# A third pair of score buffers, lent from the projection banks, in the last unit of a decoder layer

## The chip, the cores and the metric

The kernel runs on one core of a Trainium2 chip. The metric is the device time of one launch in microseconds (us). All arithmetic is fp32.

## The reference

One decoder layer for x of 4 batches x 1024 tokens x 512 features, with 16 heads of 32 features. Three blocks follow each other, each with a layer norm in front and a residual after it: a gated self-attention, a cross-attention over a context of 384 features, and a small network of 64 units with 16 hidden values each.

```python
# gated self-attention (B, H, q, k)
attn = softmax(inner @ outer.T / sqrt(dh)) * aperture[..., None] * expression[..., None, :]
attn = attn / (attn.sum(-1) + 1e-8)
x = x + rotate(attn @ v) @ Wout
# cross-attention: q from layernorm(x), k and v from the context
attn = softmax(clip(q @ k.T * D ** -0.5, -1e4, 1e4))
x = x + (attn @ v) @ Wo + bo
# network
s = layernorm(x) @ Win + bin_
g = (relu(s[..., None] * W1 + b1) * W2).sum(-1) + b2
x = x + g @ Wout + bout
```

## The kernel before, in words

The work is cut into eight **units**: self-attention of the four batches, then cross-attention of the four batches. The last unit is the cross-attention of batch 3. A unit has two **halves** of 512 queries (hf). Each half runs 32 **steps**: four groups g of four heads, and in each group eight tiles kt of 128 keys. A step (`step`, `scores`, `times`) does the following, in program order on each engine:

- TensorE computes the scores of two pairs of heads (line 574). A pair fills a tile s of 128 partitions x 2 x 512 values in PSUM, which is two banks. The pool `ps` holds two such tiles. Each head's scores are two 32x64 matmuls (16 records in a trace for the step's eight matmuls).
- ScalarE makes one exponential e for each pair (line 579), 128x1024 values, into one of six buffers.
- VectorE adds e into es, the running sum for the softmax (lines 585 and 587). In the last unit only the first pair is summed there; the second pair's row sums are TensorE matmuls, sm (line 609), made every second step for two key tiles. In the very last group of the last half (`closing`) VectorE sums both pairs, and there is no sm.
- TensorE multiplies the exponentials of the step before with the values, av (line 601).

After the last key tile of a group, `normalize` copies av and sm to SBUF (lines 618 and 620), a step later `add_up` adds the sums across partitions (line 631, copied at line 632), and their way goes by DMA: sum_d, cs, then `divide` (lines 655 to 671) three steps later, rec_d, recb, and `multiply` (line 681) after three more steps.

The other work of a unit is placed between these steps by `run(main, items)`. It has a list of small parts, each with a cost c (about one projection part is 1; pauses have a cost and no work) and gives each step its share of the list by cost. `beside(u, hf)` writes the list by hand. In the last unit, for either half, it holds: pauses; the output projection of an earlier half (line 87, 16 parts, two per step); two outputs of the network of the half before that (line 879); pauses, among which stand the layer norm (root, lines 290 to 299; normalization, line 303), its transposition by way of DMA (rows_d, line 307; xn, line 312; VectorE's block transposes, line 318) and bias additions (line 826); the inputs of the network (line 841); and pauses again. The hidden values of the network (hid on ScalarE, line 862, and g on VectorE, line 868) are spread over the pauses and the projection parts; they have no cost in the list.

All these matmuls besides scores, av and sm write to single banks that `bank()` hands out from the pool `pf`, which holds two of them (tag f). With the two tiles of `ps` (four banks) and one bank each for av and sm, all eight banks of PSUM are given out. The order on each engine is the program's; every DMA named here stands on SP's queue in program order.

After the last step of the last half, the program goes on with the last output projection, norm and network, written out by hand.

Of the kernel before, what the change touches and what calls it, by code (L numbers as in the profile page):

```python
# [10 lines left out]
F32 = mybir.dt.float32  # L11
U32 = mybir.dt.uint32
AF = mybir.ActivationFunctionType
# [3 lines left out]
P = 128  # L17
# [8 lines left out]
HALF = 512  # L26
# [4 lines left out]
SCALE = 1.0 / math.sqrt(DH)  # L31
# [32 lines left out]
def moderate_path(tc: tile.TileContext, a: dict, out: bass.AP, flag: bass.AP):  # L64
    nc = tc.nc
    x = a["x"]
    with ExitStack() as st:
# [3 lines left out]
        ps = enter(tc.tile_pool(name="mps", bufs=2, space=bass.MemoryType.PSUM))  # L71
# [5 lines left out]
        p3 = enter(tc.tile_pool(name="mp3", bufs=3))  # L77
        p4 = enter(tc.tile_pool(name="mp4", bufs=4))

        def bank():  # L80
            return pf.tile([P, HALF], F32, tag="f", name="f")

        def columns(to, lhsT, rhs, **flags):

            for j in range(4):
                r = slice(j * DH, (j + 1) * DH)
                nc.tensor.matmul(to[r], lhsT=lhsT[:, j, :] if len(lhsT.shape) == 3 else lhsT[:, r], rhs=rhs, **flags)  # L87
# [249 lines left out]
        n = len(order)  # L337
# [213 lines left out]
        def attention(u, hf):  # L551

            ph, b = order[u]
# [9 lines left out]
            def closing(g):  # L563
                return (u, hf, g) == (len(order) - 1, 1, HG - 1)

            def scores(g, kt):
                q, k = me["q", hf], me["k"]
                es = []
                for i in range(2):
                    s = ps.tile([P, 2, HALF], F32, tag="s", name="s")  # L570
                    for j in range(2):
                        r = slice((2 * i + j) * DH, (2 * i + j + 1) * DH)
                        for m in range(0, P, 64):
                            nc.tensor.matmul(  # L574
                                s[m : m + 64, j, :], lhsT=k[r, g, kt * P + m : kt * P + m + 64], rhs=q[r, g, :],
                                start=True, stop=True,
                            )
                    e = p4.tile([P, 2, HALF], F32, tag="e", name="e", bufs=6)
                    nc.scalar.activation(e, s, AF.Exp, scale=SCALE)  # L579
                    es.append(e)  # L580
                me["e", kt] = es
                for i in range(1 if shared and not closing(g) else 2):
                    if kt == 1:
                        me.setdefault("es", {})[i] = p1.tile([P, 2, HALF], F32, tag=f"es{i}", name="es")
                        nc.vector.tensor_tensor(me["es"][i], me["e", 0][i], es[i], ALU.add)  # L585
                    elif kt > 1:
                        nc.vector.tensor_tensor(me["es"][i], me["es"][i], es[i], ALU.add)  # L587
                if ph == 0 and kt > 0:
                    if kt == 1:
                        me["eg"] = p1.tile([P, 2, HALF], F32, tag="es1", name="eg")  # L590
                    for h in range(2):
                        eg, gate = me["eg"][:, h, :], lambda t: me["sw"][:, t, HG * g + h, 1:2]
                        if kt == 1:
                            nc.vector.tensor_scalar(eg, me["e", 0][0][:, h, :], gate(0), None, ALU.mult)
                        nc.vector.scalar_tensor_tensor(eg, es[0][:, h, :], gate(kt), eg, ALU.mult, ALU.add)  # L595
                return es
# [131 lines left out]
        def post(u, hf):  # L728

            ph, b = order[u]  # L730
# [22 lines left out]
            def project(t):  # L753
                def part(cs, to=None):
                    def f():
                        assert last or me["divided", hf] >= cs[-1]
                        if cs[0] == 0:
                            res["po"] = to() if to else bank()
                            res["po", t] = res["po"]
                        if last:  # L760
                            res["po"] = res["po", t]
                        for c in cs:
                            columns(
                                res["po"], me["q", hf][:, c, ts(t, P)], me["wo", hf][:, c, :],
                                start=(c == 0), stop=(c == NC - 1),
                            )
                        if cs[-1] < NC - 1:
                            return
                        r = res[t]
                        nc.vector.tensor_tensor(r, res["po"], r, ALU.add)  # L770
                        s6 = p2.tile([P, 6], F32, tag="bnst1", name="bnst1")
                        if t == 0:
                            res["mv"] = p2.tile([P, 4, 2], F32, tag="fmv", name="fmv")
                        nc.vector.bn_stats(s6, r)
                        nc.vector.bn_aggr(res["mv"][:, t, :], s6)
                        if ph == 0:
                            r2 = p2.tile([P, D], F32, tag="r2", name="r2")
                            nc.gpsimd.tensor_tensor(r2, r, bo_bc, ALU.add)  # L778
                            nc.sync.dma_start(x1b_d[b][4 * hf + t], r2)
                    return len(cs), f  # L780
                if last:
                    return [part([0, 1, 2], (lambda: ps.tile([P, 2, HALF], F32, tag="s", name="s")[:, 0, :]) if t > 1 else None), part([3])]
                return [part([c]) for c in range(4)]
# [8 lines left out]
            def root(a=0, n=4):  # L792
                if ph == 1:
                    i = 2 * NS + b * NT + 4 * hf + a
                    nc.gpsimd.tensor_copy(marks[:, i : i + n], res["mv"][:, a : a + n, 1])
                rs = rsqrt(res["mv"][:, a : a + n, :], n)
                for t in range(n):
                    res["rs", a + t] = rs[:, t : t + 1]
                if last:
                    res["nm", a] = p2.tile([P, n], F32, tag="ve", name="nm")  # L800
                    nc.vector.scalar_tensor_tensor(res["nm", a], res["mv"][:, a : a + n, 0], -1.0, rs, ALU.mult, ALU.mult)

            def norm(t):
                def f():
                    if last:
                        if t == 0:
                            res["xn"] = p1.tile([P, 4, D], F32, tag="tok", name="xn")
                        to = res["xn"][:, t, :]
                        if t % 2:
                            nc.scalar.activation(  # L810
                                to, res[t], AF.Identity, bias=res["nm", t - 1][:, 1:2], scale=res["rs", t]
                            )
                        else:
                            normalized(to, res[t], res["mv"], res["rs", t], t)
                        return
                    r2 = p2.tile([P, 1, D], F32, tag="r2", name="r2")
                    normalized(r2[:, 0, :], res[t], res["mv"], res["rs", t], t)
                    away(rows_d[b][hf], r2, t, 1)
                return [(0, f)]
# [70 lines left out]
            def bout(t):  # L890
# [11 lines left out]
            r = {  # L902
                "wo": [[(0, fetch)]],
                "load": loads,
                "o": [project(t) for t in range(4)],
                "ln": ([[(0, lambda a=a: root(a, 2))] for a in (0, 2)] if last else [[(0, root)]])
                + [norm(t) for t in range(4)],
            }
# [21 lines left out]
                done = upto  # L930
            return [out + second[done:]]

        def run(main, items):

            parts = sum(items, [])
            total = sum(c for c, _ in parts)
            done = 0
            for n, f in enumerate(main):
                f()
                while parts and (done + parts[0][0] / 2 <= total * (n + 1) / len(main) or n == len(main) - 1):  # L940
                    c, f1 = parts.pop(0)
                    if f1:
                        f1()
                    done += c
# [4 lines left out]
        n = len(order)  # L949
# [87 lines left out]
        first += one(load_wout) + one(rotations) + p["gt"][1]  # L1037
        first += p["v"][1][0:3] + pres[1]["tr"][0] + p["v"][1][3:]
        run([lambda: None], first)
        for u in range(n):  # L1040
            if u == 0:
                crossing.append(True)
            for hf in range(2):
                run(attention(u, hf), beside(u, hf))
        tail = ending[0]
        sums, divide, look = settle(n - 1, 1, HG - 1)
        late.pop(0)()
# [5 lines left out]
        o, ln, b, tr, s = ([part for item in tail[k] for part in item] for k in ("o", "ln", "b", "tr", "s"))  # L1053
        h = [part for item in held[0]["h"] for part in item]
# [18 lines left out]
        h = sum(tail["h"], [])  # L1073
# [650 lines left out]
```

## Time and profile before

| | |
|---|---|
| median of 3 runs | 2200.21 us |
| lowest and highest | 2198.55, 2200.22 us |
| profiled execution, span from first to last instruction | 2198.2 us |
| TensorE busy | 2170.0 us (99%) |
| VectorE, ScalarE, GpSimd busy | 71%, 56%, 4% |
| mean granted TensorE clock | 0.997 |
| last unit's first step, last step | 1927.8 us, 2141.6 us from the start |

The profiled execution has no time besides its span: the three times given are those of the runs. Its span lies 2.0 us under their median. In the lines of a profile PE is TensorE, PEld its weight loads, DVE is VectorE, ACT is ScalarE, SPq are DMAs issued by SP; L574 is line 574 of the kernel; "x16" counts instructions; a bracket gives idle time just before an instruction and what ended it.

### The profile page before, as it was taken

Reading aid. Unit: us, or ns where it says so; the run is one execution under the profiler, and the core shown is the slowest. Engines: PE = TensorE matmul, PEld = TensorE weight load, DVE = VectorE, ACT = ScalarE, POOL = GpSimd, SP = SyncE. Lnnn points to the kernel's source line nnn. Section 1 sums busy time; section 2 is a strip of 40 time slices with the busy share of each in tenths; the row PEclk is TensorE's granted clock in tenths of the full one; section 3 lists DMA queues with packets and bytes.
Section 4 is the critical chain, followed back from the end, with each engine's and each line's share of the span. In section 5 each row is a group of like instructions: output and inputs, shape, how many; then the busy total and the mean of one; then the engine's idle time right before and its main releaser. Section 6 shows DMA issues by size and latency. Waiting matters only on the chain.

```text
span 2198.2 us, 52765 instructions
## 1 busy us (share of the span) xinstructions
PE 2170.0 (99%) x22606; PEld 551.7 (25%) x22606; DVE 1562.5 (71%) x2526; ACT 1237.6 (56%) x1489; POOL 82.2 (4%) x118
## 2 busy tenths in 40 slices
PE   8999999999999999999999999999999999999996
PEld 3322222222222222222222222222222222222223
DVE  4478675796757957567677676877777777856477
ACT  0155545555455554555656566675757666577673
POOL 1000000030210000000000000000000000000000
PEclk9999999999999999999999999999999999999998
DMA  4412123132231221211222132222234142213131
GB/s 141 131 61 55 63 96 106 29 88 66 97 104 31 82 69 47 68 57 42 70 85 90 45 89 69 79 70 59 69 84 112 46 107 69 61 39 80 59 89 41
DMA packets 153304, 161.70 MB, mean 74 GB/s; under 512 B 46202, under 2 KB 91898, under 8 KB 151908
## 3 DMA queue, kind: packets, MB, share of 16 engines
q1 hardware_dynamic: 149068, 156.14, 24.6%
q8 instruction: 179, 2.93, 0.6%
q0 software_dynamic: 2144, 0.98, 0.3%
q10 hardware_dynamic: 1848, 1.12, 0.2%
q14 instruction: 65, 0.53, 0.1%
HBM read 115.40 MB, written 42.74 MB: 72 GB/s over the span
## 4 chain that ended last, share of the span: by engine, by line
PE 93%; DVE 3%; DMA 1%; ACT 1%; issue 1%; SPq 0%; DVEq 0%; ACTq 0%
PE f L87 36%; PE s L574 25%; PE av L601 21%; PE sm L609 6%; PE sm L631 3%; ACT e L579 1%; DMA w<-in_attn_Wo 1%; PE f L841 1%; PE f L879 1%; DVE g L868 1%; DVE es L587 1%; DMA rows_d<-r 0%; PE s L879 0%; PE f L471 0%; DMA rec_d<-rec 0%
## 5 line engine op out<-in xcount | busy, mean ns | idle before, releaser
L579 ACT ACTIVATE e<-s 128x1024 f32<-128x1024 f32 x1024 | 993.4, 1022 | 709.9 <-PE s L574 512.9
L587 DVE TENSOR_TENSOR es<-es,e 128x1024 f32<-128x1024 f32 x534 | 642.2, 1227 | 253.6 <-ACT e L579 251.6
L574 PE MATMUL s<-q,k 32*64 32x512 f32 x8192 | 607.5, 613 | 2.2 <-ACT e L579 0.5
L601 PE MATMUL av<-e,v 128*32 128x512 f32 x4096 | 550.4, 603 | 0.0
L87 PE MATMUL f<-xT,w 128*32 128x512 f32 x2816 | 333.7, 592 | 0.6 <-PE f L87 0.6
L595 DVE SCALAR_TENSOR_TENSOR eg<-e,sw,eg 128x512 f32<-128x512 f32 x448 | 318.5, 746 | 2.3
L585 DVE TENSOR_TENSOR es<-e 128x1024 f32<-128x1024 f32 x89 | 106.7, 1223 | 216.4 <-ACT e L579 185.4
L574 PEld LDWEIGHTS s<-q,k 32*64 32x64 f32 x8192 | 132.9, 130 | 445.6 <-ACT e L579 242.2
L87 PE MATMUL f<-w,q 128*32 128x512 f32 x1984 | 240.3, 593 | 0.0
L601 PEld LDWEIGHTS av<-e,v 128*32 128x32 f32 x4096 | 88.2, 108 | 403.7 <-issue 401.2
L87 PEld LDWEIGHTS f<-xT,w 128*32 128x32 f32 x2816 | 92.3, 110 | 211.0 <-issue 204.2
L609 PE MATMUL sm<-e,sw 128*2 128x512 f32 x1024 | 133.3, 592 | 0.0
L87 PE MATMUL f<-w,xT 128*32 128x512 f32 x896 | 106.0, 592 | 0.6 <-DVE q L284 0.6
L87 PEld LDWEIGHTS f<-w,q 128*32 128x32 f32 x1984 | 65.8, 110 | 148.9 <-issue 141.5
L87 PE MATMUL f<-w,ctxT 128*32 128x512 f32 x768 | 92.6, 592 | 0.0
L87 PE MATMUL f<-ctxT,w 128*32 128x512 f32 x768 | 92.3, 592 | 0.0
L862 ACT ACTIVATE hid<-sT,units 128x256 f32<-128x256 f32 x128 | 76.5, 605 | 27.9 <-DVE g L868 23.8
L778 POOL TENSOR_TENSOR r<-res,bo_bc 128x512 f32<-128x512 f32 x32 | 40.9, 1278 | 1040.7 <-DVE res L770 795.0
L868 DVE SCALAR_TENSOR_TENSOR g<-hid,units,g 128x256 f32<-128x256 f32 x120 | 57.5, 479 | 14.2 <-ACT hid L862 8.7
L631 PE MATMUL sm<-es,ones 128*1 128x512 f32 x348 | 65.0, 591 | 0.0
L770 DVE TENSOR_TENSOR res<-f,res 128x512 f32<-128x512 f32 x62 | 42.5, 685 | 18.5 <-PE f L87 9.9
L681 DVE TENSOR_TENSOR q<-both,recb 128x512 f32<-128x512 f32 x63 | 43.2, 685 | 7.0 <-DMA recb<-rec_d 7.0
(260 smaller groups left out, 1040.2 us busy)
## 6 DMA issues: line engine op xcount, KB each, us to landing
recb<-rec_d SPq DMA_DIRECT2D x252, 64.0 KB
xT<-rows_d SPq DMA_DIRECT2D x60, 256.0 KB
rows_d<-r SPq DMA_DIRECT2D x60, 256.0 KB
w<-in_xattn_Wo SPq DMA_DIRECT2D x9, 1024.0 KB
w<-wout_d SPq DMA_DIRECT2D x8, 1024.0 KB
res<-in_x SPq DMA_DIRECT2D x32, 256.0 KB
x1b_d<-r SPq DMA_DIRECT2D x32, 256.0 KB
res<-x1b_d SPq DMA_DIRECT2D x32, 256.0 KB
```

The source lines that it names most:

```text
L87: nc.tensor.matmul(to[r], lhsT=lhsT[:, j, :] if len(lhsT.shape) == 3 else lhsT[:, r], rhs=rhs, **flags)
L574: nc.tensor.matmul(s[m : m + 64, j, :], lhsT=k[r, g, kt * P + m : kt * P + m + 64], rhs=q[r, g, :], start=True, stop=True,)
L579: nc.scalar.activation(e, s, AF.Exp, scale=SCALE)
L585: nc.vector.tensor_tensor(me["es"][i], me["e", 0][i], es[i], ALU.add)
L587: nc.vector.tensor_tensor(me["es"][i], me["es"][i], es[i], ALU.add)
L595: nc.vector.scalar_tensor_tensor(eg, es[0][:, h, :], gate(kt), eg, ALU.mult, ALU.add)
L601: nc.tensor.matmul(av[r, :], lhsT=me["v"][:, kt, HG * g + h, :], rhs=es[h // 2][:, h % 2, :], start=(kt == 0), stop=(kt == NT - 1),)
L609: nc.tensor.matmul(sm[j * DH : j * DH + sums, :], lhsT=me["sw"][:, t, HG * g + 2 + h, :] if ph == 0 else ones, rhs=me["e", t][1][:, h, :], ...
L631: nc.tensor.matmul(sm[j * DH : j * DH + 1, :], lhsT=ones, rhs=e, start=True, stop=True)
L681: nc.vector.tensor_tensor(me["q", hf][:, g, :], both[:, 0, :], all_, ALU.mult)
L862: nc.scalar.activation(hid, res["s"], AF.Relu, bias=units[:, 1, h : h + 1], scale=units[:, 0, h : h + 1])
L868: nc.vector.scalar_tensor_tensor(res["g"], res["hid"], units[:, 2, h - 1 : h], res["g"], ALU.mult, ALU.add)
```

## The change

`run` looks ahead: it marks a step of the last unit as **spare** if no part with a cost and work stands just before it or just after it in the list. In a spare step, `score_banks` gives a pair of heads the two banks of the pool `pf` in place of a tile of `ps`, provided that at least two pairs went to `ps` since `bank()` was last called and that no projection is open on a bank. A call of `bank()`, by `score_banks` too, sets that count to zero, so in a row of spare steps every third pair goes to `pf`. Such a pair lies in two separate tiles of 512 values, and gets an exponential for each of them, 128x512, into the two halves of the same e. Elsewhere `score_banks` hands out the tile of `ps` as before.

```diff
+        spare = [False]
+        since = [0]
+        open_ = [0]
+
         def bank():
+            since[0] = 0
             return pf.tile([P, HALF], F32, tag="f", name="f")
+
+        def score_banks():
+
+            if spare[0] and not open_[0] and since[0] >= 2:
+                two = [bank(), bank()]
+                return two, [(slice(i, i + 1), b) for i, b in enumerate(two)]
+            since[0] += 1
+            s = ps.tile([P, 2, HALF], F32, tag="s", name="s")
+            return [s[:, i, :] for i in range(2)], [(slice(0, 2), s)]
...
                 for i in range(2):
-                    s = ps.tile([P, 2, HALF], F32, tag="s", name="s")
+                    two, reads = score_banks()
                     for j in range(2):
                         r = slice((2 * i + j) * DH, (2 * i + j + 1) * DH)
                         for m in range(0, P, 64):
                             nc.tensor.matmul(
-                                s[m : m + 64, j, :], lhsT=k[r, g, kt * P + m : kt * P + m + 64], rhs=q[r, g, :],
+                                two[j][m : m + 64], lhsT=k[r, g, kt * P + m : kt * P + m + 64], rhs=q[r, g, :],
                                 start=True, stop=True,
                             )
                     e = p4.tile([P, 2, HALF], F32, tag="e", name="e", bufs=6)
-                    nc.scalar.activation(e, s, AF.Exp, scale=SCALE)
+                    for h, s in reads:
+                        nc.scalar.activation(e[:, h, :] if len(reads) == 1 else e[:, h.start, :], s, AF.Exp, scale=SCALE)
...
                             res["po"] = to() if to else bank()
+                            open_[0] += 1
...
                         if cs[-1] < NC - 1:
                             return
+                        open_[0] -= 1
...
-        def run(main, items):
+        def run(main, items, shares=False):
 
             parts = sum(items, [])
             total = sum(c for c, _ in parts)
-            done = 0
+            done, loaded = 0, True
             for n, f in enumerate(main):
+                coming, at = False, done
+                for c, f1 in parts:
+                    if at + c / 2 > total * (n + 1) / len(main):
+                        break
+                    coming, at = coming or bool(c and f1), at + c
+                spare[0] = shares and not (loaded or coming)
                 f()
+                spare[0], loaded = False, coming
...
-                run(attention(u, hf), beside(u, hf))
+                run(attention(u, hf), beside(u, hf), shares=u + 1 == n)
```

## The prediction

> **What bounds the kernel now.** I read the busy table first, then the chain of waits for the last unit (from 1927.8 us), then that stretch's timeline and windows. The page makes TensorE look full:
>
> ```profile
> PE 2170.0 (99%) x22606; PEld 551.7 (25%) x22606; DVE 1562.5 (71%) x2526; ACT 1237.6 (56%) x1489; POOL 82.2 (4%) x118
> L579 ACT ACTIVATE e<-s 128x1024 f32<-128x1024 f32 x1024 | 993.4, 1022 | 709.9 <-PE s L574 512.9
> ```
>
> The second line is the exponential: 1022 ns for a pair of heads. The chain of waits shows that 99% busy is not 99% used. Columns are start, length, what; "x16" is one step's scores, both pairs:
>
> ```profile
> 2028.08 1.06 PE s L574 x16
> 2029.16 1.03 ACT e L579
> 2030.24 2.00 PE s L574 x16
> 2032.24 1.00 PE av L601 x8
> ```
>
> The same 16 records take 1.06 us in one step and 2.00 us in the next. When both pairs' buffers are free, the 32x64 matmuls run side by side in about 1.04 us; when the second pair waits for an exponential, each pair takes about 1.04 us alone, counted as busy throughout. With two pair buffers, pair p needs the exponential of pair p-2: the second pair of a step waits for the second exponential of the step before. Step starts in the timeline (2022.0, 2024.2, 2028.0, 2030.2, 2034.0 us) repeat every 6.02 us per two steps. TensorE work in two steps is 2x1.04 scores + 2x1.00 av + 0.86 sm (row sums, every second step) = 4.94 us. So 1.08 us per two steps is a stall for score buffers.
>
> It exists only where nothing else lies between steps. In steps with projections (3.8 to 4.6 us each) the exponentials finish in time.
>
> Two more limits lie in this unit. In the timeline of steps 16 to 24 of the second half, start first, length second:
>
> ```profile
> 2100.38 1.00 DVE L303 TENSOR_SCALAR r<-res,fmv,yi 128x512 f32<-128x512 f32 x2
> ...
> 2106.68 1.01 SPq L307 DMA_DIRECT2D rows_d<-r  x2
> ...
> 2110.74 1.92 SPq L312 DMA_DIRECT2D xn<-rows_d  x4
> ...
> 2112.76 0.43 SPq L671 DMA_DIRECT2D rec_d<-rec  x1
> ...
> 2118.33 1.71 SPq L675 DMA_DIRECT2D recb<-rec_d  x4
> ...
> 2121.70 0.69 DVE L681 TENSOR_TENSOR q<-both,recb 128x512 f32<-128x512 f32 x1 [1.64 <-DMA recb<-rec_d]
> 2122.31 1.22 DVE L587 TENSOR_TENSOR es<-es,e 128x1024 f32<-128x1024 f32 x1
> 2123.45 0.70 DVE L318 STREAM_TRANSPOSE xn<-xn 128x512 f32<-128x512 f32 x1
> 2123.49 2.64 PE L841 MATMUL f<-xn,win 128*32 128x256 f32 x32
> 2124.20 1.44 PEld L841 LDWEIGHTS f<-xn,win 128*32 128x32 f32 x28 [0.60 <-DVE xn L318]
> ```
>
> The network's input matmul (L841, after step 24) waits for the last transpose, which stands in VectorE's order behind a multiply that waits for a DMA. From the first normalization (2100.38) to the end of that transpose (2124.15) no link waits for a score. And in the last group VectorE is full (window, span, PE, PEld, DVE, ACT):
>
> ```profile
> 2018.80:2040.00 21.20, 20.84 (x202) 4.29 (x200) 12.28 (x20) 17.81 (x24) 0.00 (x0) 1.00 0.48 161
> 2128.30:2148.00 19.70, 19.70 (x180) 5.09 (x180) 19.49 (x26) 16.22 (x21) 0.00 (x0) 1.00 0.08 17
> ```
>
> VectorE is at 12.28 of 21.20 us in an ordinary stretch and at 19.49 of 19.70 us in the last group, where it makes two sums of 1.18 us a step.
>
> **What the Trainium skill says.** Perfetto Trace Analysis, "Identifying the Most-Contended Engine": matmul busy time is no measure of distance to the limit; its "Optimization Strategy" says that consistent bubbles can mean too little PSUM for the next tile. The trace agrees: 99% busy, and a bubble every 6.02 us. TensorEngine Tiling (Array Packing), "Available Configurations": 32x64 gives eight tiles; one step has just eight such matmuls, and 1.04 us for both pairs against 1.04 for one agrees. ScalarE: Activation LUTs, "What ACT_TABLE_LOAD costs": 186 ns + 0.833 ns per element with immediate operands, 93 ns overlapped back to back. For 1024 columns that is 1039 ns (trace 1022), for 512 it is 613 (the trace's 512-wide copies take 592 to 615).
>
> **The change part by part.** The lookahead in run marks a step spare if no loaded item stands before or after it. The item lists give, for either half of the last unit: two pauses and ten pauses (items 0-11), 16 projection parts (12-27), two outputs (28-31), 16 pauses (32-47), the inputs (48-49), 14 pauses; two units a step. Spare are steps 1-5, 17-23 and 26-31. The trace confirms the layout: L87 first appears after step 6 (1948.6), L841 after step 24. In each stretch a bank pair comes at pair positions 0, 3, 6, ...: 4 + 5 + 4 = 13 pairs per half, 26 in all.
>
> *ScalarE*: 26 instructions of 1024 columns become 52 of 512. Alone a half is about 0.59 us, so a pair costs 2x0.59 - 1.02 = +0.16 us if nothing overlaps. The copies at L618 and L620 start 0.47 us apart (1957.18, 1957.65) and exponentials 0.92 us apart, so overlapped it is 2x0.47 - 0.92 = +0.02; the page's price gives 2x520 - 946 = +0.09. I take +0.05 to +0.1; the ends are 0 and 0.17. Behind them on ScalarE wait hid and the copies of both. A two-step cycle with hid holds 4x0.92 + 2x0.5 = 4.7 us of ScalarE, 4.8 with the split, under TensorE's 4.94, so it is nearly hidden, with little to spare.
>
> *TensorE*: buffers now recur after three pairs. A step's first pair needs an exponential finished long ago, its second the first exponential of the step before: score start + 1.15 + 1.02 + 0.05 = 2.2 us, where a step without sm lasts 2.04. The residue is about 0.2 us every second step: cycle 4.94 + 0.2 = 5.15 instead of 6.02, 0.87 saved. I carried this from step to step with the trace's durations (score 1.04, av 1.00, sm 0.86, exponentials 0.92 apart, hid 0.5); the same arithmetic with two buffers gives the trace's starts within 0.2 us. The results:
> - first half, steps 1-6 (step 6 gains too, since its buffers come free sooner): 1930.04 to 1948.62 becomes 16.1 us from 1929.85: **2.5 saved**.
> - first half, steps 26-31, into step 0 of the second: **2.0 saved**.
> - second half, steps 1-6 (2040.04 to 2057.98): **1.9 saved**.
> - steps 17-24, both halves: TensorE would come to L841 about 2 us sooner (2.6 in the second, where it waits already), but the transposes end at 2013.99 and 2124.15 as before. What goes on the score buffers returns as a wait of L841: 0 saved. A split exponential ahead of the copy L632 delays the sum_d DMAs, behind which rows_d stands on SP, by up to 0.1: **-0.2** in all.
> - second half, steps 26-31: VectorE's sums from 2128.26 to 2147.99 set the end, and the tail's divisions follow on VectorE: 0.
>
> Sum: 2.5 + 2.0 + 1.9 - 0.2 = 6.2 us. Projections of steps 6-16 take banks only after the exponentials that av needs anyway; no DMA is added, and no queue is passed. The multiply that the second projection step needs is done at 1946.75, needed at 1952.4, so 2.5 us less lead is covered. Of the bookkeeping (since, open_, spare) nothing reaches the chip; other units keep their instructions.
>
> The profiled execution spans 2198.2 us, the runs' median is 2200.21, 2.0 more. I take the 6.2 from the median: 2194.0.
>
> **Rivals.**
> - *The DMA chain gives way* (16%). If SP's issues move forward with the steps, steps 17-24 gain about 2 + 2.6 and the last group up to 2: 8 to 13 us, 2187 to 2192. For it: add_up and divide are due by step count. Against: their rec_d DMA (2112.76) stands on SP behind the xn load, itself waiting for rows_d. DMA: Bandwidth & Descriptors, "Anatomy of one DMA", puts such waits at the issuing sequencer and the fixed cost at 2.0 us; the trace shows 5.6 us from rec_d to recb.
> - *ScalarE takes the gain* (17%). If halves don't overlap and hid falls behind a late exponential, cycles come to 5.4 to 5.8 us; gain 1 to 4 us, 2196 to 2199. That also covers a lost stretch, and a change that does nothing because the banks are never offered: 2200.2.
> - *ScalarE becomes the bound* (5%). It decides once a bank pair costs more than (6.02 - 4.7) / 1.33 = 1.0 us extra, 1.33 pairs falling in a cycle. At 1.5 us the cycle is 6.7; 0.7 x 8 cycles of the three effective stretches = 5.5 us slower, 2205.7. Only a table reload or a long wait between halves could do it; the page shows three table loads in all.
>
> **How the numbers follow.** The likeliest case (62%) is 2194.0, with 2191.5 to 2196 from the split's bounds and DMA scatter. The range 2188.5 to 2197.5 takes in most of the first two rivals. A measurement tells 0.2%, 4.4 us, from no change: faster means under 2195.8. Faster 0.77 (most of the likeliest, and the first rival), same 0.18, slower 0.05.
>
> **What would show it.** L579 as 998 instructions of 1024 columns and 52 of 512, mean 570 to 620 ns. Score groups of 2.00 us gone from steps 1-6 of both halves and 26-31 of the first. A wait of L841's weight load for the transpose of about 2 us in each half. VectorE as full as now in the last group. Wrong if L841 doesn't wait, if ScalarE is full between the steps, or if step 7 of either half starts no sooner.

## The result and the profile after

The changed kernel takes 2195.83 us (median of 11 runs, 2190.75 to 2199.55), the kernel before 2200.22 us in the same measurement (11 runs, 2198.55 to 2201.30). The ratio is 0.9978, its 95% interval 0.9969 to 0.9986: 3.1 to 6.8 us faster. Measured a second time, the pair gave 2194.42 (14 runs, 2191.65 to 2199.60) against 2199.72, ratio 0.9978 [0.9970, 0.9986]. The prediction said 2194.0, from 2188.5 to 2197.5.

The profiled execution of the kernel after took 2196.38 us, of which 2194.6 are its span. In the page after (busy us, share, instructions; then the largest group of section 5):

```profile
PE 2162.4 (99%) x22606; PEld 551.4 (25%) x22606; DVE 1562.1 (71%) x2526; ACT 1238.7 (56%) x1515; POOL 82.2 (4%) x118
...
L594 ACT ACTIVATE e<-s 128x1024 f32<-128x1024 f32 x998 | 969.8, 1022 | 695.3 <-PE s L588 493.5
```

TensorE has the same 22606 matmuls, and lost 7.6 us of busy time though no matmul was removed: most of it is time of score pairs that ran one after the other and now run side by side (about 7 us in the last unit, by the table below). ScalarE has 26 instructions more, as 26 exponentials became 52. The groups by form, over the last unit, show these (count, busy us, mean ns). In traces of the kernel after, line 594 is the exponential, and scores in the lent banks have the name f:

```profile
L594 ACT ACTIVATE e<-f 128x512 f32<-128x512 f32 x52 | 28.3, 603 | 2.7 <-PE s L588 2.5
```

603 ns a half, where the prediction said 570 to 620. The chain of waits, from step 28 of the first half into the second (start, length, what), answers to the one shown of before:

```profile
2024.45 1.21 PE s L588 x16
...
2027.52 0.59 PE f L588 x4
2028.10 0.03 PE s L588 x4
2028.13 0.40 PE f L588 x4
2028.53 0.03 PE s L588 x4
2028.56 0.99 PE av L616 x8
...
2033.72 1.03 ACT e L594
...
2034.80 2.00 PE s L588 x16
```

Steps now cost 1.05 to 1.21 us of scores. A step with a bank pair (f and s mixed) is no exception: its four pieces from 2027.52 to 2028.56 add up to 1.05. In steps 1 to 6 of both halves, too, no step's scores take longer than 1.34 us from first start to last end. Only one group of 2.00 us is left here, at step 0 of the second half, which is not a spare step and whose scores must wait for an exponential (2033.72). The windows of the first stretch, the step 26 stretch and the last group (span, PE, PEld, DVE, ACT, POOL, clock, DMA share, GB/s) are:

```profile
1931.10:1949.40 18.30, 18.30 (x208) 4.33 (x208) 11.11 (x17) 16.65 (x27) 0.00 (x0) 1.00 0.07 18
2019.50:2036.80 17.30, 17.18 (x190) 3.75 (x192) 12.01 (x20) 16.29 (x26) 0.00 (x0) 1.00 0.32 103
2124.20:2144.10 19.90, 19.23 (x184) 5.04 (x182) 19.44 (x26) 16.61 (x26) 0.00 (x0) 1.00 0.08 16
```

ScalarE is at 16.65 of 18.30 us in the first: close to full, not full. VectorE is at 19.44 of 19.90 us in the last group, as before. Against the kernel before, TensorE starts step 25 3.86 us sooner and step 31 5.10, but VectorE's last sum (line 602) ends only 3.82 us sooner: what TensorE gains in the group goes no further. And a wait is new, which the waits of TensorE list for 1990 to 2130 us (total, times, longest):

```profile
PE f L858 <- DVE xn L332: 3.0, 2, 1.8
```

The network's input matmul (line 858, before: 841) waits for the last transpose of its input, 1.22 us in the first half and 1.78 in the second. The kernel before had no entry there; only weight loads waited, 0.60 us at most. The second half in the timeline:

```profile
2117.85 0.69 DVE L696 TENSOR_TENSOR q<-both,recb 128x512 f32<-128x512 f32 x1 [1.77 <-DMA recb<-rec_d]
...
2118.45 1.22 DVE L602 TENSOR_TENSOR es<-es,e 128x1024 f32<-128x1024 f32 x1
...
2119.59 0.70 DVE L332 STREAM_TRANSPOSE xn<-xn 128x512 f32<-128x512 f32 x1
...
2120.35 1.92 PE L858 MATMUL f<-xn,win 128*32 128x256 f32 x28 [1.78 <-DVE xn L332]
```

Read upward: the matmul waits for a transpose, which stands behind a sum, which stands behind the multiply (line 696), which waits 1.77 us for a DMA. No link of it is a score buffer.

**Where the time went.** The table gives, for the same TensorE instruction in two traces, its start in the kernel named less its start in the kernel before (us; minus is sooner). "h1" and "h2" are the halves of the last unit, and a number is the step whose first scores are meant. "End" is the start of the last matmul.

| kernel | unit starts | h1 17 | h1 26 | h2 0 | h2 7 | h2 17 | h2 25 | end |
|---|---|---|---|---|---|---|---|---|
| after | +3.28 | +0.75 | +0.62 | -1.46 | -3.55 | -3.55 | -3.86 | -4.37 |
| after, second time | +0.01 | -2.51 | -2.72 | -4.79 | -6.88 | -6.87 | -6.56 | -6.57 |
| e1_no_middle | +0.43 | -2.10 | -2.09 | -4.16 | -6.25 | -6.25 | -2.52 | -5.00 |
| e2_middle_only | +0.26 | +0.26 | +0.09 | +0.09 | +0.09 | +0.10 | -0.52 | -1.01 |
| e3_split_only | -0.13 | -0.07 | +0.13 | +0.26 | +0.39 | +0.39 | +0.49 | -2.18 |
| e7_three_stretches | -0.08 | -2.60 | -2.60 | -4.67 | -6.76 | -6.76 | -6.33 | -9.09 |
| e6_half_sums | -0.06 | -2.58 | -2.82 | -4.89 | -6.98 | -6.98 | -7.58 | -9.33 |
| e10_multiply_later | +0.20 | -2.32 | -5.16 | -6.94 | -9.42 | -9.42 | -9.08 | -11.84 |

The first profile after is 3.28 us late before the last unit begins, in code that the change doesn't touch. Its timeline shows where, 62 us from the start:

```profile
59.91 2.49 DVE L332 STREAM_TRANSPOSE xT<-xT 128x512 f32<-128x512 f32 x4 [2.20 <-DMA xT<-rows_d]
...
62.51 4.05 PE L101 MATMUL f<-xT,w 128*32 128x512 f32 x20 [2.12 <-DVE xT L332]
```

A DMA landed later than in the profile before, so that TensorE stood for 2.12 us (0.58 in the profile before), and then ran at half clock for 3.4 us (the clock is the column after POOL):

```profile
62.90:66.30 3.40, 3.40 (x20) 1.09 (x16) 0.08 (x1) 0.00 (x0) 0.00 (x0) 0.50 0.00 0
```

The second profile of the same kernel has neither, and starts the last unit at +0.01. So one must subtract along a row of the table, never compare whole spans.

### The profile page after: what moved, and what is told of

Same layout as the page of the kernel before. It is cut to its first block, busy times and chain, and to the rows that moved or that the text cites. A ratio compares the mean times of both kernels' runs of the same rounds, so it can differ in the third digit from the quotient of the medians.

```text
span 2194.6 us, 52792 instructions
## 1 busy us (share of the span) xinstructions
PE 2162.4 (99%) x22606; PEld 551.4 (25%) x22606; DVE 1562.1 (71%) x2526; ACT 1238.7 (56%) x1515; POOL 82.2 (4%) x118
## 4 chain that ended last, share of the span: by engine, by line
PE 91%; DVE 3%; DMA 2%; issue 1%; ACT 1%; SPq 0%; DVEq 0%; ACTq 0%
PE f L101 36%; PE s L588 24%; PE av L616 21%; PE sm L624 6%; PE sm L646 3%; DVE es L602 1%; ACT e L594 1%; PE f L858 1%; PE f L896 1%; DVE g L885 1%; DMA rec_d<-rec 1%; DMA rows_d<-r 0%; DMA xT<-rows_d 0%; PE f L485 0%; PE f L1054 0%
## 5 line engine op out<-in xcount | busy, mean ns | idle before, releaser
L594 ACT ACTIVATE e<-s 128x1024 f32<-128x1024 f32 x998 | 969.8, 1022 | 695.3 <-PE s L588 493.5
L588 PE MATMUL s<-q,k 32*64 32x512 f32 x7984 | 595.0, 613 | 1.4 <-ACT e L594 0.8
```

The source lines that it names most:

```text
L588: nc.tensor.matmul(two[j][m : m + 64], lhsT=k[r, g, kt * P + m : kt * P + m + 64], rhs=q[r, g, :], start=True, stop=True,)
L594: nc.scalar.activation(e[:, h, :] if len(reads) == 1 else e[:, h.start, :], s, AF.Exp, scale=SCALE)
```

## The experiments

The theory under test is the prediction's: a gain in three stretches, none in steps 17 to 24 and none in the last group. Each kernel below is the kernel after with the edit shown, and its ratio is to the kernel before on the same chip.

**e1_no_middle: no bank pairs in steps 17 to 23.**

```diff
-                spare[0] = shares and not (loaded or coming)
+                spare[0] = shares and not (loaded or coming) and not 17 <= n <= 23
```

> The changed kernel with the bank pairs left out of steps 17 to 23 of both halves; steps 1 to 5 and 26 to 31 keep them. My theory: what the middle steps gain ends as a wait of the network's input matmul for the last transpose, so leaving them out costs nothing: 2192 to 2196 us, and the wait before that matmul (1.2 and 1.8 us in the changed kernel's profile) falls under 0.8 us in both halves. A second part of it: the changed kernel's runs scatter by 8.8 us (2190.75 to 2199.55) because idle stretches of TensorE of some 2 us bring a 3.4 us window at half clock, so without those waits the scatter shrinks to under 5 us and the granted clock is 0.997 or more in every run. The rival that the chain of DMAs gives way with the steps expects 3 to 4.6 us more than the changed kernel, 2198 to 2200.

Measured: 2194.05 us (9 runs, 2193.47 to 2195.34), ratio 0.9973 [0.9963, 0.9983]. The row of e1 has the same 2.53 us up to h1 17 and the same 2.07 and 2.09 around h2 0 as the kernel after: the ten pairs left out carried none of the gain. In the first half the wait of line 858 is gone. In the second it is longer than expected:

```profile
PE f L858 <- DVE xn L332: 2.4, 1, 2.4
```

In this execution the multiply waited 3.04 us for recb (2117.78), with the steps ahead of it unchanged; the wait in front of line 858 then cost 3.7 us from h2 17 to h2 25, for it was followed by 3.4 us at half clock (from 2120.7 on). That part of the expectation was missed. The spread of 1.9 us is as small as expected, but the wait that was to be its cause is still there, and the granted clock is 0.996 in three of the nine runs, where 0.997 or more was expected.

**e2_middle_only: the reverse, bank pairs in steps 17 to 23 alone.**

```diff
-                spare[0] = shares and not (loaded or coming)
+                spare[0] = shares and not (loaded or coming) and 17 <= n <= 23
```

> The changed kernel with the bank pairs in steps 17 to 23 of both halves alone. My theory: no gain, 2199.5 to 2202 us, waits of 1.2 to 2 us before the network's input matmul in both halves, and scattered runs if those waits bring half-clock windows. The rival that the chain of DMAs gives way expects 2195 to 2197 us and no such waits.

Measured: 2201.15 us (13 runs, 2198.38 to 2205.78), ratio 1.0009 [1.0001, 1.0018]: no gain, and rather 1.0 us slower. Line 858 waits 1.19 and 1.47 us:

```profile
PE f L858 <- DVE xn L332: 2.7, 2, 1.5
```

From step 17 to step 24 TensorE comes 2.20 us earlier in either half (in the first from +0.26 to -1.94 in the table's terms). Behind the inputs 0.2 and 0.6 us of it are left. So the middle's saving exists, and nearly all of it is lost at the inputs, 2.7 us of it as the waits shown. Together, e1 and e2 show it from both sides.

**e3_split_only: the 26 exponentials split, the score buffers as before.**

```diff
-                two = [bank(), bank()]
-                return two, [(slice(i, i + 1), b) for i, b in enumerate(two)]
+                since[0] = 0
+                s = ps.tile([P, 2, HALF], F32, tag="s", name="s")
+                return [s[:, i, :] for i in range(2)], [(slice(i, i + 1), s[:, i, :]) for i in range(2)]
```

> The same 26 pairs get two exponentials of 512 columns each, but their scores stay in tiles of the pool with two pair buffers: the split without the third buffer. My theory: in the changed kernel's profile a split pair takes 1.08 us for 1.02 and starts its follower 0.97 instead of 0.92 us later; where an exponential ends late it releases the buffer late, which the two-buffer ring feels once per two steps: 0 to 1.5 us slower than before, 2200 to 2202. The rival that the split takes much of the gain on ScalarE expects 2 to 4.5 us slower, 2202 to 2205. Nothing gained in any case unless the first half's earlier end frees something: then 2198 to 2199.5.

Measured: 2200.96 us (13 runs, 2198.78 to 2204.16), ratio 1.0007 [0.9998, 1.0015]. In the trace the unit loses 0.62 us from its start to h2 25 (-0.13 to +0.49). Without the third buffer the split costs under a microsecond, and nothing is gained: the gain is the buffer's.

**e7_three_stretches: bank pairs only where the prediction counted a gain.** 12 pairs are left of 26, four in each stretch; the expectation counts one too many.

```diff
-                spare[0] = shares and not (loaded or coming)
+                spare[0] = shares and not (loaded or coming) and not 17 <= n <= 23 and not (n > 23 and ending)
```

> Bank pairs only in the three stretches that the prediction counted: steps 1 to 5 of both halves and 26 to 31 of the first; 13 pairs instead of 26. My theory: the last group gains nothing from them, so the time is e1's, 2193 to 2195 us, with as small a scatter (under 3 us). A rival by which the last group loses with the split exponentials on ScalarE: 0.5 to 1.5 us faster than e1. One by which it gains: 1.5 to 2 us slower.

Measured: 2193.69 us (7 runs, 2191.04 to 2194.03), ratio 0.9971 [0.9960, 0.9982]. The row has 2.52, 2.07 and 2.09 us in the three stretches and 0.4 lost in h2 17 to 25; the wait of line 858 is 0.5 us. Twelve of the 26 pairs bring the whole gain. The 2.8 us between h2 25 and the end are the tail's, of which below.

**e6_half_sums: is it VectorE that sets the last group?** Here VectorE sums only the first pair of heads there, and both pairs' row sums are taken from that sum: this part of the computation is changed.

```diff
-                for i in range(1 if shared and not closing(g) else 2):
+                for i in range(1 if shared else 2):
...
-                        sm[j * DH : (j + 1) * DH, :], lhsT=ones.to_broadcast([P, DH]), rhs=me["es"][j // 2][:, j % 2, :],
+                        sm[j * DH : (j + 1) * DH, :], lhsT=ones.to_broadcast([P, DH]), rhs=me["es"][0][:, j % 2, :],
```

> The changed kernel, but in the very last group VectorE sums only the first pair's exponentials (the second pair's sums are left out, the first pair's stand in for them). My theory that VectorE's two sums a step (2.35 us) set the last group: with one sum the group's steps go at 5.1 to 5.3 us per two steps instead of 5.2 to 5.7 and the divisions start 2 to 3 us sooner: 2192 to 2194 us. If TensorE or ScalarE sets the last group: within 0.7 us of the changed kernel, 2195 to 2196.5.

Measured: 2191.46 us (6 runs, 2190.41 to 2195.50), ratio 0.9967 [0.9955, 0.9979], a little faster than expected and 4.4 and 3.0 us below the two medians of the kernel after, though the intervals overlap. The trace is clearer. The window of the last group, cut at the same places in VectorE's order as the one shown of the kernel after (from 0.2 us before the first sum to just before the end of the last):

```profile
2120.48:2136.49 16.01, 15.72 (x160) 3.62 (x158) 11.95 (x19) 16.01 (x26) 0.00 (x0) 1.00 0.08 19
```

With VectorE at 11.95 us, the group takes 16.0 instead of 19.9 us, and now ScalarE is full, at 16.01 us. So VectorE set the group, and its bank pairs had nothing to give as the kernel stands. Not all of the 3.9 us reaches the end of the program: from h2 25 to the end the row gains 1.75 us.

**e4_late_inputs: turn the wait of line 858 into a gain, by placing the inputs one step later.**

```diff
-                out += weave(last["tr"], pause(3)) + last["s"] + weave(some(last, 8), pause(14))
+                out += weave(last["tr"], pause(3)) + pause(2) + last["s"] + weave(some(last, 8), pause(12))
```

> The changed kernel with the network's inputs one step later in the list of either half of the last unit (two pauses ahead of them, two fewer behind). My theory: the input matmul then comes after the transposes, TensorE no longer waits there, and the steps 17 to 24 keep what the third buffer gives them: 1 to 2 us in the first half, 1.5 to 2.5 in the second (where VectorE's sums of the last group can start that much sooner), so 2189 to 2193 us and a scatter under 5 us with the clock at 0.997 or more. The rival that VectorE or the tail is the limit in the second half expects 2193 to 2195; if the hidden values, squeezed into fewer steps, become late, the same or slower than the changed kernel.

Measured: 2195.27 us (13 runs, 2193.41 to 2198.16), ratio 0.9980 [0.9971, 0.9988]: no better than the kernel after, and short of the 2189 to 2193 expected. The shift also moves the spare steps, so that there are 28 bank pairs. In the first half it works: TensorE gains 1.86 us from h1 17 to h1 26 (-2.30 to -4.16), where the kernel after gained 0.13; a wait of 0.97 us is left, of line 646. In the second half a longer wait comes in its place, then another one:

```profile
2114.47 0.69 DVE L696 TENSOR_TENSOR q<-both,recb 128x512 f32<-128x512 f32 x1 [2.27 <-DMA recb<-rec_d]
...
2115.24 0.59 ACT L633 COPY both<-av 128x512 f32<-128x512 f32 x1 [2.88 <-issue]
...
2116.44 0.60 PE L646 MATMUL sm<-es,ones 128*1 128x512 f32 x2 [3.04 <-ACT both L635]
...
2132.57 0.60 ACT L879 ACTIVATE hid<-sT,units 128x256 f32<-128x256 f32 x1 [2.57 <-DVE g L885]
...
2134.13 1.97 PE L588 MATMUL s<-q,k 32*64 32x512 f32 x8 [2.44 <-ACT e L594]
```

TensorE's sum matmul (line 646) waits 3.04 us for a copy that stands behind the copy of line 633, and this starts only once the multiply has read its buffer `both`. Later the hidden values, pressed into fewer steps beside a full VectorE, hold up ScalarE for 2.57 us and through it the scores for 2.44. After the first of these two stops TensorE ran at half clock for 3.4 us, after the second for 6.8 us.

**e5_free_both: is it the buffer, or the multiply itself?** On top of e4, the copy of av goes straight to its slice of q in the last unit and is multiplied in place, so that `both` is no longer waited for.

```diff
-                nc.scalar.copy(both[:, 0, :], av)
+                nc.scalar.copy(me["q", hf][:, g, :] if u + 1 == len(order) else both[:, 0, :], av)
...
-                nc.vector.tensor_tensor(me["q", hf][:, g, :], both[:, 0, :], all_, ALU.mult)
+                av_ = me["q", hf][:, g, :] if u + 1 == len(order) else both[:, 0, :]
+                nc.vector.tensor_tensor(me["q", hf][:, g, :], av_, all_, ALU.mult)
```

> The changed kernel with the inputs one step later, as in e4, and in the last unit normalize copies av straight into the group's slice of q (its scores are done) where multiply then scales it in place, so the buffer both no longer waits for the multiply and its DMA. In e4's profile the wait for the transposes had become a wait of 3.0 us (second half) and 1.0 us (first) of the sums of add_up for ScalarE's copy, which waited for that multiply. My theory: with both gates moved the steps 17 to 24 keep their gain of about 2 us per half up to the last group, no gap of TensorE over 1 us from 1930 us to the last group; first half 1.5 to 2.5 us better than e1, the second likewise unless VectorE's last group takes it: 2189 to 2193 us. The rival that the last group on VectorE is the end anyway: 2192 to 2194, with the gain visible in the trace until 2120 us and gone by 2150.

Measured: 2195.01 us (12 runs, 2192.49 to 2197.08), ratio 0.9977 [0.9969, 0.9986], again short of the 2189 to 2193 expected. The first half gains 1.92 us from h1 17 to h1 26, as in e4. In the second half the wait only changes its name, and grows:

```profile
2114.40 0.69 DVE L697 TENSOR_TENSOR q<-q,recb 128x512 f32<-128x512 f32 x1 [2.97 <-DMA recb<-rec_d]
2115.01 1.22 DVE L602 TENSOR_TENSOR es<-es,e 128x1024 f32<-128x1024 f32 x1
...
2116.37 0.60 PE L646 MATMUL sm<-es,ones 128*1 128x512 f32 x2 [3.31 <-DVE es L602]
```

The sum that line 646 reads stands behind the multiply on VectorE. The gate of the second half is thus the multiply: while it waits for recb, everything behind it on VectorE stands, sums and transposes alike.

**e8_fill_wait: do half-clock stretches explain the scatter?** The kernel after's runs spread over 8.8 us, those of before over 2.75. Two idle matmuls are put ahead of the inputs, so that TensorE does not stand there.

```diff
+                    if (u, hf) in ((n - 2, 1), (n - 1, 0)):
+                        idle = bank()
+                        for i in range(2):
+                            nc.tensor.matmul(idle, lhsT=ident, rhs=wout, start=True, stop=True)
```

> The changed kernel with two idle matmuls of 128x128 by 512 columns (about 0.86 us each) just ahead of the network's inputs in the last unit, where TensorE waits for the transposes; their result is used by nothing. If the scatter and the missing 1.7 us of the changed kernel come from half-clock windows that idle stretches of about 2 us bring: 2193.5 to 2195 us, scatter under 5 us, no half-clock window between 1930 us and the tail. If they come from DMA landing late or from the tail: same median and scatter as the changed kernel, 2195.5 to 2197.5.

Measured: 2193.95 us (9 runs, 2190.16 to 2195.31), ratio 0.9971 [0.9961, 0.9981]. Its trace has no gap over 0.7 us in the last unit and no half-clock stretch there, and its median is where the half-clock theory had it. But its interval overlaps with that of the kernel after, and its runs spread over 5.2 us where under 5 were expected. Inconclusive.

**e9_again and e10_multiply_later: the same kernel a second time, and a version built on the finding.** In e10 the multiply, too, is moved behind the transposes: in the first half the multiply of group 1 comes two steps later and the inputs one step later, with av copied into q as in e5. The second half, where the last group follows at once, keeps its order and has bank pairs in steps 1 to 5 only; 18 pairs are left.

```diff
-                nc.scalar.copy(both[:, 0, :], av)
+                nc.scalar.copy(me["q", hf][:, g, :] if u + 1 == len(order) else both[:, 0, :], av)
...
-                after(apart(g), lambda: multiply(g, both, all_), behind=u + 1 < len(order))
+                after(apart(g) + (2 if (u, hf, g) == (len(order) - 1, 0, 1) else 0), lambda: multiply(g, both, all_), behind=u + 1 < len(order))
...
-                nc.vector.tensor_tensor(me["q", hf][:, g, :], both[:, 0, :], all_, ALU.mult)
+                av_ = me["q", hf][:, g, :] if u + 1 == len(order) else both[:, 0, :]
+                nc.vector.tensor_tensor(me["q", hf][:, g, :], av_, all_, ALU.mult)
...
-                spare[0] = shares and not (loaded or coming)
+                spare[0] = shares and not (loaded or coming) and not (n > 16 and ending)
...
-                out += weave(last["tr"], pause(3)) + last["s"] + weave(some(last, 8), pause(14))
+                out += weave(last["tr"], pause(3)) + (pause(2) if hf == 0 else []) + last["s"] + weave(some(last, 8), pause(14 if hf else 12))
```

> The changed kernel once more, unaltered, on the chip of e10, for its scatter and for the comparison with the versions without the middle steps (2194.05 and 2193.69 us) and with filled waits (2193.95). If idle waits at the network's inputs cost it something beyond them: a median of 2195 to 2197 us with a scatter over 6 us. If it is equal to those versions: 2193.5 to 2194.5 us with a scatter under 4 us.

> A candidate. Bank pairs in steps 1 to 5 of both halves and in all spare steps of the first; in the first half the network's inputs one step later, and the multiply of group 1 (the one that stops VectorE until recb has landed) two steps later, with av copied straight into q so that nothing waits for that multiply. My theory, that the gate is this multiply in VectorE's order with the transposes behind it: the first half's steps 17 to 24 keep their gain, 2.0 to 2.9 us beyond e7 (trace offset against the kernel before near 2014 us of -5 to -5.6 instead of -2.6, with no gap of TensorE over 0.7 us there), the second half is as in e7; 2190.5 to 2192 us, scatter under 4 us. If the DMA chain itself (xn) is the gate, a gap of 0.5 to 1.5 us stays and the time is 2192 to 2193.5.

Measured: e9_again as given at the top; its median fits the second of its two expectations and its spread of 8.0 us the first, so it decides for neither. e10: 2190.60 us (5 runs, 2188.64 to 2191.21), ratio 0.9960 [0.9947, 0.9974]; 3.8 below the kernel after on the same chip: each of its five runs is faster than each of the fourteen of the kernel after. Its first half in the timeline:

```profile
2007.46 1.18 DVE L602 TENSOR_TENSOR es<-es,e 128x1024 f32<-128x1024 f32 x1
...
2008.57 0.70 DVE L332 STREAM_TRANSPOSE xn<-xn 128x512 f32<-128x512 f32 x1
...
2009.29 0.69 DVE L697 TENSOR_TENSOR q<-q,recb 128x512 f32<-128x512 f32 x1
...
2011.84 1.90 PE L859 MATMUL f<-xn,win 128*32 128x256 f32 x28
```

The transpose is ahead of the multiply, no bracket shows an idle time, and from h1 17 to h1 26 the row gains 2.84 us where the kernel after gained 0.13. Of this, e4 and e5 had 1.86 and 1.92 by the later inputs (which give step 24 a bank pair, too); the later multiply brings the other 0.9 to 1.0 us. The saving of the middle steps was real, and held back in the first half by the order of the transposes, the multiply and the inputs. What e10's order would do in the second half, no run here shows.

## Why the prediction was right

Its terms, each as a difference of two columns in the table:

| term | predicted | after | second time | e7 |
|---|---|---|---|---|
| first half, steps 1-6 (start to h1 17) | 2.5 | 2.53 | 2.52 | 2.52 |
| first half, middle (h1 17 to 26) | about -0.1 | 0.13 | 0.21 | 0.00 |
| first half, steps 26-31 (h1 26 to h2 0) | 2.0 | 2.08 | 2.07 | 2.07 |
| second half, steps 1-6 (h2 0 to 17) | 1.9 | 2.09 | 2.08 | 2.09 |
| second half, middle (h2 17 to 25) | about -0.1 | 0.31 | -0.31 | -0.43 |
| sum | 6.2 | 7.14 | 6.57 | 6.25 |

- **The stall and its size.** Right, term by term within 0.2 us. The arithmetic of three buffers, carried from step to step with the trace's durations, holds on the chip.
- **The middle steps.** Right: the gain returned as a wait of line 858, "about 2 us" for the weight load by the prediction. The two weight loads waited 4.0 us in all, the longer 2.3, and TensorE's matmuls 1.22 and 1.78, behind the transposes. e1 and e2 show it. The small loss by delayed DMAs is not confirmed: the middle changed by -0.43 to +0.31 us, and the -0.43 is e7's, which splits no exponential there.
- **The split.** A pair of halves takes 1.08 us where a whole exponential takes 1.02, and the exponential behind it starts 0.97 instead of 0.92 us later: +0.05, the lower end of what the prediction took. In all it cost about 0.6 us (e3).
- **The last group.** Right: VectorE, by e6, and by the last sum of the kernel after, which gained nothing in the group.
- **The rivals.** The DMA chain did not give way (line 858 waits, e4 and e5 show what for), ScalarE did not take the gain, and it did not become the bound (0.05 us extra a pair against the 1.0 from which it would).
- **What was not foreseen.** Up to h2 25 the last unit gained 7.1 and 6.6 us in the two traces of the kernel after, the medians 4.4 and 5.3. What differs lies outside the sum: the runs of the kernel after scatter over 8.8 and 8.0 us, those of before over 2.8 and 3.3, and its first profile lost 3.28 us in untouched code. One source of such losses is seen in the traces: a stop of TensorE that is followed by a half-clock stretch. The mean clocks of its runs point the same way: of the kernel after's 25 runs, the four at 0.995 took 2197.8 to 2199.6 us and the seven at 0.998 took 2190.8 to 2194.9; a clock lower by 0.003 over 2195 us is an estimated 6.6 us of TensorE's work. But how much of the scatter the waits of line 858 explain is open: e1 and e7 spread over 1.9 and 3.0 us, but e3, which has no such wait, over 5.4, and e8 without such stops in the unit can't be told from the kernel after. The two medians and 6.2 are within one interval of each other, so no difference of the sum from the measurement is proved either.

The prediction put nothing for the tail, from h2 25 to the end, and that can't be read from one trace: in kernels that leave it untouched it gave -0.1 to 2.8 us (e3 2.67, e7 and e10 2.76, the second profile 0.01, e8 -0.09). TensorE stops for 2.1 us at its beginning, before line 339 (before: 325). In e1, e3, e7 and e10, the four with 2.5 to 2.8 us, no half clock followed this stop; in all other traces, that of the kernel before included, a half-clock stretch began within 2.3 us of its end. So the tail's difference goes with where the half clock falls, which no run here moves on purpose. Why it follows one stop and not another is taken up at the end.

## What to carry to other kernels

A TensorE that is 99% busy can still be stalled: compare how long the same group of matmuls takes in neighbouring steps, and count PSUM buffers against the exponentials that free them. Lend idle buffers only in the steps whose end nothing else sets; here 12 of the 26 lent pairs brought the whole gain. Where a saving runs into a wait, look not only at what the waiting engine waits for but at what stands ahead of that in its own engine's order: moving only the matmul that waited brought 1.9 us in the first half and a longer wait in the second, and moving the DMA-bound multiply behind the transposes as well brought 2.8 in the first.

## What was not expected of the hardware

Half-clock stretches followed stops of TensorE that were shorter than thought. The Trainium skill, TensorE: Matmul & The Clock Gate, "Part 1: The HAM clock gate (the "warmup" mystery)", has the clock fall to half after at least one idle window of about 3.4 us, in windows that run free of the kernel. The length agrees: the stretches inside these traces last 3.4 us or twice that. The free-running windows agree too: within each trace all changes of the clock lie on one grid of 3.41 us (in e5 the stretches begin at 2117.7, 2134.8, 2165.5, 2182.6 and 2189.4 us, which is 5, 9, 5 and 2 times 3.41 apart). But the window need not be wholly idle: 2.12 us of standing still (after, up to 62.5 us) and 2.44 us (e1, up to 2120.3 us) were each followed by half clock, while 2.40 us at the same place in the second profile of the kernel after was not, and the stops of 1.1 to 1.8 us at that place, in the kernel after, e2 and e6, never were.

The traces show what differs. Cut along each trace's own grid, the windows around these stops are, for the kernel after, e1, e5 (a stop of 3.31 us) and the second profile of the kernel after (span, then PE):

```profile
59.49:62.90 3.41, 1.29 (x16) 0.19 (x8) 2.98 (x5) 0.00 (x0) 0.00 (x0) 1.00 0.39 129
...
2117.25:2120.66 3.41, 0.97 (x16) 0.40 (x14) 2.45 (x3) 1.07 (x2) 0.00 (x0) 1.00 0.00 0
...
2114.31:2117.72 3.41, 1.35 (x16) 0.55 (x18) 2.67 (x4) 1.30 (x2) 0.00 (x0) 1.00 0.00 0
...
2112.30:2115.72 3.42, 2.95 (x28) 0.60 (x20) 1.56 (x3) 1.65 (x2) 0.00 (x0) 1.00 0.23 82
2115.72:2119.13 3.41, 1.48 (x26) 0.91 (x28) 1.87 (x3) 1.07 (x2) 0.00 (x0) 1.00 0.00 0
```

The first three held 1.35 us of TensorE work or less, and half clock began at their ends. In the last case the grid cuts the stop of 2.40 us into 0.4 and 2.0 us, and none followed. From 20 us to the tail, in all twelve traces, each window with 2.1 us or more of standing was followed by half clock, and none with 2.0 or less. In the tail the bound is less clean: there 1.86 us was enough in e1, e3, e7 and e10. So a stop of about 2 us can be followed by 3.4 us at half clock, 1.7 us of work, or not, by where the grid cuts it, and this makes a wait of 2 us dearer than it looks in a chain of waits.
